# Layer 0's side work placed gap by gap, by the time that each burst of scores leaves

## The chip, the cores and the metric

The kernel runs on one core of a Trainium2 chip, as one program of 39,772 recorded instructions. The metric is the device time of one execution in microseconds (us). It is the median of three runs: 2475.52 us, from 2474.48 to 2475.53.

The engines are TensorE (PE in the profile; PEld is its weight load), VectorE (DVE), ScalarE (ACT), GpSimd (POOL) and SyncE (SP), which issues the DMAs.

## The reference

Four layers of attention run one after the other on `x` (4 batches, 1024 rows, 256 columns, 16 heads of 16) and a context of 77 rows per batch, all in f32. The change is in layer 0, which is causal attention over the layer's own rows and the context, then a feed-forward part:

```python
def _L0_xattn_ref(x, context, ...):
    qkv = (_ln(x, g1, be1) @ w_qkv + b_qkv).reshape(b, t, 3, h, dh)
    ckv = (context @ w_ckv + b_ckv).reshape(b, s, 2, h, dh)
    k = concatenate([k_self, k_ctx], axis=1); v = concatenate([v_self, v_ctx], axis=1)
    scores = where(causal_or_context, einsum('bthd,bshd->bhts', q, k) * scale, -inf)
    x = x + einsum('bhts,bshd->bthd', softmax(scores), v).reshape(b, t, d)
    hdn = gelu(_ln(_ln(x, g2, be2), gf, bf) @ w1 + b1, approximate=False)
    return x + (hdn @ w2 + b2)
```

Layer 1 is a linear attention on the context beside a windowed attention on the rows. Layers 2 and 3 are cross attention to the context, layer 2 with a mask and weights on the scores and a layer norm behind it.

## The kernel before

Layers 0 and 1 work on *units*: four heads of one batch, a "quad", so 16 units a layer. Layer 0 is one call of `step` for each unit (L1634 to L1648). A step runs two things at once: the row maxima of its own unit (`Max0`, eleven items from the table `MAX0`) and the exponentials and sums of the unit before (`Sum0`, twelve items). An item's score products go to a PSUM tile `ps` of two banks. An item has two parts p of two heads each.

`step` (L496) makes a list of bursts of the items: one item of each kind gives two bursts, each with one part of both. A step has 23 bursts, the first step of all (no unit before it) 11. `burst` (L472) issues the products for two `ps` tiles, row by row in turn, then what reads them (`take`): a `tensor_reduce` on DVE into `mpart` (L601) for a `Max0`, an `Exp` on ACT into `pe` (L666) for a `Sum0`, with an `affine_select` on POOL (L669) on the diagonal. The pool `big` holds two `ps` tiles, so a burst can start when both tiles of the burst before it have been read.

Behind each burst comes a *gap*. In it stand, in this order: `sums` of the burst before where it ended an item (products of `pe` and the values into `pv`, L45); what was deferred (transposes `pm` and `pt` of the maxima and of the sums); and a share of the *jobs*. A job is a generator that does one piece of other work for each `next`: `heads0` (queries and keys of the units to come through `project_eight` into `pp`, copied on ACT at L364 and spread by DMA into `qk`), `values0` (`ppv`), `context0`, `ffn` (the feed-forward part of an earlier batch, `ph` and `po`), `ffn_norms`, `features0`, and work for later layers (`folded2`, `keys2`, `heads3`, `keys3`, `folded3`). Each piece takes one or two buffers of the PSUM pool `sm`, which has three.

How far a job has to be is set by `Job.run`: with n pieces and a window a to b of the step, it does pieces until `did` has reached n x (share - a)/(b - a). `share` is how much of the step's sum of `needs` has gone by; a burst's need is a number from its columns, at least 160. All jobs are brought up to the share in the order of the list, so a gap gets as many pieces as fall due there. `jobs0` lists the jobs of each step of layer 0, `jobs1` those of layer 1. The calls to SP's queue (`nc.sync.dma_start`) stand inside the pieces and are issued in the same order.

Layer 1 uses the same `step`, `gap` and `Job`. Layers 2 and 3 use `Job.run` alone, through `gap2`.

Of the kernel before, what the change touches and what calls it, by code (L numbers as in the profile page):

```python
# [31 lines left out]
def tile_xattn_seq(ctx: ExitStack, tc: tile.TileContext, d: dict, out: bass.AP):  # L32
# [8 lines left out]
    sm = ctx.enter_context(tc.tile_pool(name="sm", bufs=3, space=bass.MemoryType.PSUM))  # L41
    pvp = ctx.enter_context(tc.tile_pool(name="pv", bufs=1, space=bass.MemoryType.PSUM))

    def mm(o, lhsT, rhs, start=True, stop=True, **kw):
        nc.tensor.matmul(o, lhsT, rhs, start=start, stop=stop, **kw)  # L45


# [138 lines left out]
            yield  # L186

    ffw = {}

    def load_w1():  # L190
        ffw[1] = wpool.tile([P, 2, FF], F32, name="w1", tag="s3")
# [156 lines left out]
                    )  # L348
                yield None

    def project_eight(st, w, half, xT, bias):

        for q in range(2):
            pp = sm.tile([P, 512], F32, name="pp", tag="sm")
            for c in range(2):
                mm(
                    pp, w[:, c, P * half : P * half + P], xT[:, c, 512 * q : 512 * q + 512],
                    start=(c == 0), stop=(c == 1),
                )
            o = st[:, 512 * q : 512 * q + 512]  # L360
# [75 lines left out]
    class Job:  # L436


        def __init__(self, gen, n, a=0.0, b=1.0, rest=False):
            self.gen, self.n, self.a, self.b, self.did, self.rest = gen, n, a, b, 0, rest  # L440

        def run(self, share):
            want = self.n * min(1.0, max(0.0, (share - self.a) / (self.b - self.a)))
            while self.did < want - 1e-6:
                self.did += 1
                if next(self.gen, StopIteration) is StopIteration:
                    break

        def end(self):
# [35 lines left out]
    def step(items, jobs):  # L485


        bursts = []
        behind = 0
        for m, t in items:  # L490
            cols = max(i.cols for i in (m, t) if i)
            if m and t:
                for p in range(2):
                    bursts.append(((m, p), (t, 1 - p), p and t, cols, p * behind))
            else:
                one = m or t  # L496
                bursts.append(((one, 0), (one, 1), t, 2 * cols, behind if t else 0))
# [12 lines left out]
        for j in jobs:  # L510
            j.end()
# [208 lines left out]
    def heads0(b, half, dst):  # L720


        def begin(quad):
            u = dst[0, b, quad] = new_unit(b, quad)
            u["va"], u["vc"] = vas[half], vcs[b % 2]
            spread(u["kT"][:, 0:S], shared["kc", b][:, half, :], quad % 2)
            return u["qT"], u["kT"][:, S:]

        sts = stage()
        to = begin(2 * half)  # L730
        xT = shared["xT0", b]
        for k in range(2):
            yield from project_eight(
                sts[k], wqk0[:, k], half, xT, bqk0[:, 2 * k + half : 2 * k + half + 1]
            )
# [64 lines left out]
    def ffn(b):  # L800
# [5 lines left out]
        for q in range(5):  # L806
            for half in range(2):
                if q < 4:
                    h = hs[q, half] = work.tile([P, 4, D], F32, name="hT", tag="hT", bufs=3)
                    for f in range(4):  # L810
                        ph = sm.tile([P, D], F32, name="ph", tag="sm")
                        fs = slice(P * (4 * half + f), P * (4 * half + f + 1))
                        for c in range(2):
                            mm(
                                ph, ffw[1][:, c, fs], yT[:, c, D * q : D * q + D],
                                start=(c == 0), stop=(c == 1),
                            )
# [369 lines left out]
    def heads1(b, half, dst):  # L1187
# [13 lines left out]
        to = begin(2 * half)  # L1201
        xT = shared["xT1", b]
        for k, w in enumerate((l1["wq"], l1["wwk"])):
            yield from project_eight(sts[k], w, half, xT, None)
            spread(to[k][:, 0:T], sts[k], 0)
        to = begin(2 * half + 1)
        for k in range(2):
# [319 lines left out]
    def jobs0(b, quad):  # L1527
# [6 lines left out]
            more_places()  # L1534
        if b == 0 and quad == 0:
            j.append(Job(later_constants(), 3, 0.0, 0.4))
            j.append(Job(keep("c00", None), 1, 0.1, 0.2))
# [3 lines left out]
            j.append(Job(values2(), 2, 0.1, 0.2))  # L1541
            j.append(Job(folded2(), 24, 0.2, 1.0))
            j.append(Job(keys2(), 4, 0.5, 0.9))
        if (b, quad) == (0, 1):
            j.append(Job(heads3("wk"), 8, 0.0, 1.0))
        if (b, quad) == (0, 2):
            j.append(Job(keys3(), 16, 0.0, 1.0))
        if (b, quad) == (0, 3):
            j.append(Job(heads3("wv"), 8, 0.0, 1.0))
        if (b, quad) in ((1, 0), (1, 1)):  # L1550
            j.append(Job(keep("f3", folded3), 15 - 6 * quad, 0.0, 1.0, quad == 1))
        if quad == 0 and b + 1 < NB:
            j.append(Job(stats0(b + 1), 8, 0.3 if b == 0 else 0.0, 1.0))
        if quad == 1:
            j.append(Job(values0(b, 1), 4, 0.15, 0.95))
            j.append(Job(keep(("h0", b, 1), lambda: heads0(b, 1, units)), 4, 0.0, 0.85))
            if b:
                j.append(Job(ffn_norms(b - 1), 24, 0.2, 1.0))
        if quad == 2:
# [6 lines left out]
                j.append(Job(features1(0), 8, 0.62, 1.0))  # L1566
        if quad == 3:
            if b + 1 < NB:
                j.append(Job(values0(b + 1, 0), 4, 0.15, 0.9))
                j.append(Job(context0(b + 1), 2, 0.0, 0.4))  # L1570
                j.append(Job(keep(("h0", b + 1, 0), lambda: heads0(b + 1, 0, units)), 4, 0.15, 0.85))
            else:
                j.append(Job(context1(0), 3, 0.3, 0.5))
                j.append(Job(values1(0, 0), 4, 0.4, 0.95))
                j.append(Job(keep(("h1", 0, 0), lambda: heads1(0, 0, units)), 4, 0.45, 0.85))
# [53 lines left out]
    for _ in range(4):  # L1629
        next(run4)  # L1630
    prev = []
    for b in range(NB):
        for quad in range(4):
# [13 lines left out]
            step(pair_up(maxima0(u), prev), jobs0(b, quad))  # L1647
            prev = weights0(u)  # L1648
    shared["st8", 0, 1] = stage()
    for b in range(NB):  # L1650
        for quad in range(4):
            u = units[1, b, quad]
# [96 lines left out]
```

## Time and profile before

| what | value |
|---|---|
| median of three runs | 2475.52 us |
| the profiled execution: its own time | 2472.59 us |
| its span, first to last instruction | 2470.9 us |
| mean granted TensorE clock | 0.972 |
| layer 0's first and last `pe` | 114.1 and 1264.2 us |
| HBM read, written | 57.70 MB, 20.59 MB |

The page's costliest groups (line, engine, operation, output <- input, shapes, count; then busy us, mean ns of one; then the engine's idle time just before them and what ended most of it):

```profile
L45 PE MATMUL ps<-qk 32*128 32x192 f32 (+8 forms) x5760 | 616.5, 468 | 102.1 <-DVE mpart L601 54.4
L666 ACT ACTIVATE pe<-ps 128x1024 f32<-128x1024 f32 (+2 forms) x384 | 363.2, 952 | 612.2 <-PE ps L45 607.0
L601 DVE TENSOR_REDUCE mpart<-ps 128x2 f32<-128x1024 f32 (+3 forms) x448 | 409.0, 933 | 349.1 <-PE ps L45 348.7
```

A line can be that of a helper: all of PE's products but the transposes are recorded at L45, in `mm`. So the tile's name tells what a product is for. "Idle before" of an engine that waits for the bottleneck costs nothing; PE's own idle time does.

### The profile page before, as it was taken

The page shows a single profiled execution, that of the slowest core. Times are in us where ns is not written, and L with a number is a line of the kernel's source. Part 1 is how long each engine was busy: PE and PEld are TensorE (multiplying, and loading weights), DVE is VectorE, ACT ScalarE, POOL GpSimd, SP SyncE. Part 2 cuts the span into 40 slices and gives each one's busy share as a digit, 9 for nine tenths or more (in the row PEclk, how much of TensorE's full clock was granted, in tenths as well). Part 3 has the DMA queues.
Part 4 walks back from the last instruction along what each step waited for, and adds up shares of the span by engine and source line. Part 5 has one row for each costly group of instructions (what it writes and reads, how often), then busy time and mean ns, then how long its engine had stood idle before and what let it go on. Part 6 is the DMA issues. An engine that isn't in the chain of part 4 may idle for free.

```text
span 2470.9 us, 39772 instructions
## 1 busy us (share of the span) xinstructions
PE 2284.0 (92%) x16162; PEld 1376.6 (56%) x16162; DVE 1398.5 (57%) x2347; ACT 1033.3 (42%) x1716; POOL 640.5 (26%) x923
## 2 busy tenths in 40 slices
PE   5789989898998989989999999999997999899999
PEld 3433434344444544445456766666654777788887
DVE  4446456654466444665436345454436899776664
ACT  1244344344344334433453343444444677532222
POOL 2011013111131111311134223333341366643222
PEclk9699999999999999999999999999998999999999
DMA  6402021100000000010000100111104334022200
GB/s 176 115 25 93 6 72 41 45 6 14 1 6 15 6 14 2 5 35 5 14 6 14 19 16 15 19 19 19 19 1 151 124 120 133 28 52 57 54 14 18
DMA packets 87136, 98.49 MB, mean 40 GB/s; under 512 B 31222, under 2 KB 77866, under 8 KB 86826
## 3 DMA queue, kind: packets, MB, share of 16 engines
q1 hardware_dynamic: 86954, 95.95, 14.5%
q8 instruction: 128, 2.10, 0.4%
q14 instruction: 54, 0.44, 0.1%
HBM read 57.70 MB, written 20.59 MB: 32 GB/s over the span
## 4 chain that ended last, share of the span: by engine, by line
PE 78%; DVE 11%; ACT 6%; issue 2%; POOL 1%; DMA 1%; SPq 1%; ACTq 0%; DVEq 0%; POOLq 0%
PE ps L45 33%; PE po L45 15%; PE pp L45 6%; PE pv L45 5%; DVE mpart L601 5%; PE ph L45 4%; PE ppv L45 2%; PE psT L1285 2%; PE pvw L45 2%; ACT pe L666 2%; PE ptx L338 1%; PE pvl L45 1%; PE pk L45 1%; PE pt L542 1%; PE pm L525 1%
## 5 line engine op out<-in xcount | busy, mean ns | idle before, releaser
L45 PE MATMUL ps<-qk 32*128 32x192 f32 (+8 forms) x5760 | 616.5, 468 | 102.1 <-DVE mpart L601 54.4
L666 ACT ACTIVATE pe<-ps 128x1024 f32<-128x1024 f32 (+2 forms) x384 | 363.2, 952 | 612.2 <-PE ps L45 607.0
L601 DVE TENSOR_REDUCE mpart<-ps 128x2 f32<-128x1024 f32 (+3 forms) x448 | 409.0, 933 | 349.1 <-PE ps L45 348.7
L45 PEld LDWEIGHTS ps<-qk 32*128 32x128 f32 (+1 forms) x5760 | 288.2, 185 | 375.0 <-DVE mpart L601 134.1
L45 PE MATMUL po<-U,pT 128*128 128x256 f32 (+1 forms) x1280 | 290.5, 382 | 7.4 <-DVE x L1405 4.7
L45 PEld LDWEIGHTS po<-U,pT 128*128 128x128 f32 (+1 forms) x1280 | 239.8, 191 | 50.0 <-ACT pT L1286 8.0
L669 POOL TENSOR_SCALAR_AFFINE_SELECT pe<-pe 128x256 f32<-128x256 f32 (+1 forms) x192 | 95.0, 495 | 637.0 <-ACT pe L666 636.1
L1056 DVE TENSOR_REDUCE mrow<-ps 128x4 f32<-128x768 f32 x128 | 122.5, 957 | 141.4 <-PE ps L45 141.0
L1286 ACT COPY pT<-psT 128x512 f32<-128x512 f32 (+1 forms) x192 | 92.0, 517 | 228.1 <-PE psT L1285 228.0
L1131 ACT ACTIVATE pew<-ps 128x768 f32<-128x768 f32 x128 | 103.4, 811 | 173.4 <-PE ps L45 172.6
L1136 POOL TENSOR_SCALAR_AFFINE_SELECT pew<-pew 128x512 f32<-128x512 f32 x128 | 81.6, 637 | 342.0 <-ACT pew L1131 342.0
L45 PE MATMUL pv<-pe,va 128*32 128x512 f32 (+3 forms) x1536 | 165.0, 518 | 0.1
L45 PE MATMUL ps<-G,xT 128*128 128x308 f32 x512 | 143.0, 423 | 0.0
L45 PE MATMUL ph<-yT,w 128*128 128x256 f32 x512 | 138.1, 405 | 0.8 <-DVE qk L527 0.8
L1366 ACT ACTIVATE s<-s,nm 128x77 f32<-128x77 f32 x512 | 131.2, 352 | 15.9 <-DVE nm L1399 15.9
L1498 POOL TENSOR_TENSOR s<-s,den 128x1232 f32<-128x1232 f32 x32 | 72.0, 2249 | 207.7 <-DVE den L1497 192.4
L45 PEld LDWEIGHTS ph<-yT,w 128*128 128x128 f32 x512 | 93.6, 198 | 52.6 <-issue 39.1
L45 PE MATMUL po<-w,hT 128*128 128x256 f32 x512 | 117.0, 382 | 0.0
L45 PEld LDWEIGHTS ps<-G,xT 128*128 128x128 f32 x512 | 92.4, 190 | 26.8
L45 PEld LDWEIGHTS po<-w,hT 128*128 128x128 f32 x512 | 95.4, 190 | 21.0 <-issue 9.1
L527 DVE TENSOR_TENSOR qk<-pm,qk 128x512 f32<-128x512 f32 x64 | 44.0, 688 | 105.2 <-PE pm L525 105.2
L818 DVE TENSOR_SCALAR hT<-ph,c_L_xattn_b 128x256 f32<-128x256 f32 x128 | 61.3, 480 | 72.4 <-PE ph L45 65.2
(191 smaller groups left out, 3175.7 us busy)
## 6 DMA issues: line engine op xcount, KB each, us to landing
side<-in_fside_t SPq DMA_DIRECT2D x32, 616.0 KB
qk<-st SPq DMA_DIRECT2D x256, 64.0 KB
U<-kept_u SPq DMA_DIRECT2D x8, 1152.0 KB
side<-in_mask_t SPq DMA_DIRECT2D x32, 154.0 KB
G<-kept_g SPq DMA_DIRECT2D x4, 1232.0 KB
x<-in_x SPq DMA_DIRECT2D x8, 512.0 KB
out<-x SPq DMA_DIRECT2D x32, 128.0 KB
kept_u<-st SPq DMA_DIRECT2D x21, 154.0 KB
```

Source lines behind the costliest of these rows:

```text
L45: nc.tensor.matmul(o, lhsT, rhs, start=start, stop=stop, **kw)
L601: nc.vector.tensor_reduce(mpart[bl][:, i, 2 * p : 2 * p + 2, ci], ps[:, :, o : o + w], axis=AX.X, op=ALU.max,)
L666: nc.scalar.activation(pp[:n, :, o:512], ps[:n, :, o:512], AF.Exp, scale=SC)
L669: nc.gpsimd.affine_select(out=own, in_=own, compare_op=ALU.is_ge, fill=0.0, base=0, pattern=[[0, 2], [0, k], [1, P]], channel_multiplier=-1,)
L818: nc.vector.tensor_scalar(h[:, f, :], ph, cols["L0_xattn_b1"][:, 4 * half + f : 4 * half + f + 1], None, ALU.add,)
L1056: nc.vector.tensor_reduce(mo, ps.rearrange("p j (i n) -> p j i n", i=2)[:, :, :, 0 : P + WIN], axis=AX.X, op=ALU.max, negate=True,)
L1131: nc.scalar.activation(pp[:, :, :, 0 : P + WIN], ps.rearrange("p j (i n) -> p j i n", i=2)[:, :, :, 0 : P + WIN], AF.Exp, scale=SC,)
L1136: nc.gpsimd.affine_select(out=pf[:, :, 0:P], in_=pf[:, :, 0:P], compare_op=ALU.is_ge, fill=0.0, base=0, pattern=[[0, 4], [1, P]], channel_ ...
L1285: nc.tensor.transpose(ps[:, k, :], s[:, P * c : P * c + P], ident)
L1286: nc.scalar.copy(pT[:, 4 * group : 4 * group + n, :], ps[:, 0:n, :])
L1366: nc.scalar.activation(hs, hs, AF.Exp, bias=p1["nm"][:, h : h + 1], scale=SC)
L1498: nc.gpsimd.tensor_tensor(s3, s3, den.unsqueeze(2).to_broadcast([P, H, S]), ALU.mult)
```

## The change

Layer 0's jobs that use PE get a cost of one piece in us (`us=`); the others keep `us=0` and run as before. `mm` counts what was put on PE, in `put`, as columns / 600. `step` works out, where there are jobs with a cost, how long each burst's tiles are read beyond what stands in the gap anyway (`reads`), and raises or lowers all of them by one amount `lo` so that they sum to the work of the jobs. Each gap then takes pieces with a cost in `fill`: always the job that is furthest behind, in us, until nothing is behind or the gap's time is used up; a job that is more than two pieces and 1 us behind is served anyway. What a gap leaves over or overdraws goes to the next through `left`.

Two kinds of piece are halved in layer 0: `project_eight` works on 256 columns in place of 512 (8 pieces per `heads0` in place of 4; layer 1 keeps 512), and the second product of `ffn` on 128 columns in place of 256, with its own add on DVE for each half; `whole` turns this off once layer 1 begins.

```diff
+    put = [0.0]
     def mm(o, lhsT, rhs, start=True, stop=True, **kw):
+        n = 1
+        for k in rhs.shape[1:]:
+            n *= k
+        put[0] += n / 600.0
         nc.tensor.matmul(o, lhsT, rhs, start=start, stop=stop, **kw)
...
-    def project_eight(st, w, half, xT, bias):
-        for q in range(2):
-            pp = sm.tile([P, 512], F32, name="pp", tag="sm")
+    def project_eight(st, w, half, xT, bias, n):
+        for q in range(T // n):
+            pp = sm.tile([P, n], F32, name="pp", tag="sm")
...
+        def late(self, share):
+            want = self.n * min(1.0, max(0.0, (share - self.a) / (self.b - self.a)))
+            return want - self.did
+        def piece(self):
+            self.did += 1
+            return next(self.gen, StopIteration) is not StopIteration
...
         for j in jobs:
-            j.run(share)
+            if not j.us:
+                j.run(share)
+    def fill(share, jobs, until):
+        while True:
+            due = [(j.late(share) * j.us, -i) for i, j in enumerate(jobs) if j.us and j.did < j.n]
+            late, i = max(due, default=(-1.0, 0))
+            if late <= 1e-6:
+                break
+            j = jobs[-i]
+            if late < 2.0 * j.us + 1.0 and put[0] + 0.5 * j.us > until:
+                break
+            if not j.piece():
+                j.did = j.n
...
-        needs = [max(160.0, 140 + cols - 0.8 * filled) for *_, cols, filled in bursts]
-        total, at = sum(needs), 0.0
-        for (*parts, t, _, _), need in zip(bursts, needs):
+        work = sum(j.n * j.us for j in jobs)
+        if work:
+            reads = [0.3 + n * (0.1 + c / 455.0) - f / 600.0 for *_, n, c, f in bursts]
+            lo, hi = -3.0, 30.0
+            for _ in range(40):
+                more = (lo + hi) / 2
+                if sum(max(0.0, r + more) for r in reads) > work:
+                    hi = more
+                else:
+                    lo = more
+            needs = [max(0.0, r + lo) for r in reads]
+        else:
+            needs = [max(160.0, 140 + n * c - 0.8 * f) for *_, n, c, f in bursts]
+        total, at, left = sum(needs), 0.0, 0.0
+        for (*parts, t, _, _, _), need in zip(bursts, needs):
             burst([(i, p, pair_tile()) for i, p in parts])
             if t and pending:
                 pending.pop(0)()
             at += need
+            left += need
+            was = put[0]
             gap(at / total, jobs)
+            fill(at / total, jobs, was + left)
+            left -= put[0] - was
...
-                        po = sm.tile([P, D], F32, name="po", tag="sm")
-                        for f in range(8):
-                            mm(
-                                po, h2[f // 4][:, f % 4, P * i : P * i + P], ffw[2][:, f, :],
-                                start=(f == 0), stop=(f == 7),
-                            )
-                        nc.vector.tensor_tensor(xq, po, xq, ALU.add)
-                        nc.gpsimd.tensor_tensor(xq, xq, rows["b2"], ALU.add)
-                        for _ in range(4):
-                            yield
+                        n = D if whole else P
+                        for a in range(0, D, n):
+                            po = sm.tile([P, n], F32, name="po", tag="sm")
+                            for f in range(8):
+                                mm(
+                                    po, h2[f // 4][:, f % 4, P * i : P * i + P],
+                                    ffw[2][:, f, a : a + n], start=(f == 0), stop=(f == 7),
+                                )
+                            nc.vector.tensor_tensor(xq[:, a : a + n], po, xq[:, a : a + n], ALU.add)
+                            if a + n == D:
+                                nc.gpsimd.tensor_tensor(xq, xq, rows["b2"], ALU.add)
+                            for _ in range(n // 64):
+                                yield
...
-            j.append(Job(values0(0, 0), 4, 0.2, 0.8))
+            j.append(Job(values0(0, 0), 4, 0.2, 0.8, us=0.85))
...
-            j.append(Job(keep(("h0", b, 1), lambda: heads0(b, 1, units)), 4, 0.0, 0.85))
+            j.append(Job(keep(("h0", b, 1), lambda: heads0(b, 1, units)), 8, 0.0, 0.85, us=0.85))
...
-                j.append(Job(keep(("ffn", fb), lambda: ffn(fb)), n, a, 0.97, last))
+                j.append(Job(keep(("ffn", fb), lambda: ffn(fb)), n, a, 0.97, last, us=0.85))
```

The other jobs of `jobs0` get their `us` in the same way: `folded2`, `folded3` and the first context 0.85, `context0` 0.9, `values2` 1.0, `keys2` 0.5, `heads3` and `keys3` 1.03, `heads1` (four pieces still) 1.7. Without a cost stay `stats0`, `features0`, `ffn_norms`, `ffn_features`, `stats1`, `features1`, `context1`, the constants, and the last piece of `heads0`, which loads the keys of the next unit in the first gap of every second step.

More of the change, by code (lines that the diff above doesn't have):

```diff
@@ L188, in tile_xattn_seq @@
     ffw = {}
+    whole = []
     def load_w1():
@@ L349, in to_features @@
                 yield None
-    def project_eight(st, w, half, xT, bias):
-        for q in range(2):
-            pp = sm.tile([P, 512], F32, name="pp", tag="sm")
+    def project_eight(st, w, half, xT, bias, n):
+        for q in range(T // n):
+            pp = sm.tile([P, n], F32, name="pp", tag="sm")
             for c in range(2):
                 mm(
-                    pp, w[:, c, P * half : P * half + P], xT[:, c, 512 * q : 512 * q + 512],
+                    pp, w[:, c, P * half : P * half + P], xT[:, c, n * q : n * q + n],
                     start=(c == 0), stop=(c == 1),
                 )
-            o = st[:, 512 * q : 512 * q + 512]
+            o = st[:, n * q : n * q + n]
             if bias is None:
@@ L436, in tile_xattn_seq, with __init__ @@
     class Job:
-        def __init__(self, gen, n, a=0.0, b=1.0, rest=False):
+        def __init__(self, gen, n, a=0.0, b=1.0, rest=False, us=0.0):
             self.gen, self.n, self.a, self.b, self.did, self.rest = gen, n, a, b, 0, rest
+            self.us = us
+        def late(self, share):
[4 more added lines that the diff above has]
+            return next(self.gen, StopIteration) is not StopIteration
         def run(self, share):
[L443 to L446, printed above, removed]
+            while self.late(share) > 1e-6:
+                if not self.piece():
                     break
@@ L493, in step @@
                 for p in range(2):
-                    bursts.append(((m, p), (t, 1 - p), p and t, cols, p * behind))
+                    bursts.append(((m, p), (t, 1 - p), p and t, 1, cols, p * behind))
             else:
                 one = m or t
-                bursts.append(((one, 0), (one, 1), t, 2 * cols, behind if t else 0))
+                bursts.append(((one, 0), (one, 1), t, 2, cols, behind if t else 0))
             if t:
                 behind = t.cols
-        needs = [max(160.0, 140 + cols - 0.8 * filled) for *_, cols, filled in bursts]
-        total, at = sum(needs), 0.0
-        for (*parts, t, _, _), need in zip(bursts, needs):
+        work = sum(j.n * j.us for j in jobs)
[13 more added lines that the diff above has]
+        for (*parts, t, _, _, _), need in zip(bursts, needs):
             burst([(i, p, pair_tile()) for i, p in parts])
@@ L733, in heads0 @@
             yield from project_eight(
-                sts[k], wqk0[:, k], half, xT, bqk0[:, 2 * k + half : 2 * k + half + 1]
+                sts[k], wqk0[:, k], half, xT, bqk0[:, 2 * k + half : 2 * k + half + 1], D
             )
@@ L1203, in heads1 @@
         for k, w in enumerate((l1["wq"], l1["wwk"])):
-            yield from project_eight(sts[k], w, half, xT, None)
+            yield from project_eight(sts[k], w, half, xT, None, 512)
             spread(to[k][:, 0:T], sts[k], 0)
@@ L1536, in jobs0 @@
             j.append(Job(later_constants(), 3, 0.0, 0.4))
-            j.append(Job(keep("c00", None), 1, 0.1, 0.2))
-            j.append(Job(values0(0, 0), 4, 0.2, 0.8))
+            j.append(Job(keep("c00", None), 1, 0.1, 0.2, us=0.85))
+            j.append(Job(values0(0, 0), 4, 0.2, 0.8, us=0.85))
             j.append(Job(other_contexts(), 3, 0.0, 0.1))
             j.append(Job(feature_weights(), 3, 0.5, 1.0))
-            j.append(Job(values2(), 2, 0.1, 0.2))
-            j.append(Job(folded2(), 24, 0.2, 1.0))
-            j.append(Job(keys2(), 4, 0.5, 0.9))
+            j.append(Job(values2(), 2, 0.1, 0.2, us=1.0))
+            j.append(Job(folded2(), 24, 0.2, 1.0, us=0.85))
+            j.append(Job(keys2(), 4, 0.5, 0.9, us=0.5))
         if (b, quad) == (0, 1):
-            j.append(Job(heads3("wk"), 8, 0.0, 1.0))
+            j.append(Job(heads3("wk"), 8, 0.0, 1.0, us=1.03))
         if (b, quad) == (0, 2):
-            j.append(Job(keys3(), 16, 0.0, 1.0))
+            j.append(Job(keys3(), 16, 0.0, 1.0, us=1.03))
         if (b, quad) == (0, 3):
-            j.append(Job(heads3("wv"), 8, 0.0, 1.0))
+            j.append(Job(heads3("wv"), 8, 0.0, 1.0, us=1.03))
         if (b, quad) in ((1, 0), (1, 1)):
-            j.append(Job(keep("f3", folded3), 15 - 6 * quad, 0.0, 1.0, quad == 1))
+            j.append(Job(keep("f3", folded3), 15 - 6 * quad, 0.0, 1.0, quad == 1, us=0.85))
         if quad == 0 and b + 1 < NB:
@@ L1554, in jobs0 @@
         if quad == 1:
-            j.append(Job(values0(b, 1), 4, 0.15, 0.95))
-            j.append(Job(keep(("h0", b, 1), lambda: heads0(b, 1, units)), 4, 0.0, 0.85))
+            j.append(Job(values0(b, 1), 4, 0.15, 0.95, us=0.85))
+            j.append(Job(keep(("h0", b, 1), lambda: heads0(b, 1, units)), 8, 0.0, 0.85, us=0.85))
             if b:
@@ L1568, in jobs0 @@
             if b + 1 < NB:
-                j.append(Job(values0(b + 1, 0), 4, 0.15, 0.9))
-                j.append(Job(context0(b + 1), 2, 0.0, 0.4))
-                j.append(Job(keep(("h0", b + 1, 0), lambda: heads0(b + 1, 0, units)), 4, 0.15, 0.85))
+                j.append(Job(values0(b + 1, 0), 4, 0.15, 0.9, us=0.85))
+                j.append(Job(context0(b + 1), 2, 0.0, 0.4, us=0.9))
+                j.append(Job(keep(("h0", b + 1, 0), lambda: heads0(b + 1, 0, units)), 8, 0.15, 0.85, us=0.85))
             else:
                 j.append(Job(context1(0), 3, 0.3, 0.5))
-                j.append(Job(values1(0, 0), 4, 0.4, 0.95))
-                j.append(Job(keep(("h1", 0, 0), lambda: heads1(0, 0, units)), 4, 0.45, 0.85))
+                j.append(Job(values1(0, 0), 4, 0.4, 0.95, us=0.85))
+                j.append(Job(keep(("h1", 0, 0), lambda: heads1(0, 0, units)), 4, 0.45, 0.85, us=1.7))
         for fb, n, a, last in (
@@ L1628, in tile_xattn_seq @@
     run4 = keep(("h0", 0, 0), lambda: heads0(0, 0, units))
-    for _ in range(4):
+    for _ in range(8):
         next(run4)
@@ L1649, in tile_xattn_seq @@
     shared["st8", 0, 1] = stage()
+    whole.append(True)
     for b in range(NB):
```

## The prediction

> **What bounds the kernel now.** I read the page first, then the waits of TensorE (PE) between 115 and 1200 us, which is layer 0 without its start, then the timeline of PE there, then short windows for the clock.
>
> ```profile
> span 2470.9 us, 39772 instructions
> ...
> PE 2284.0 (92%) x16162; PEld 1376.6 (56%) x16162; DVE 1398.5 (57%) x2347; ACT 1033.3 (42%) x1716; POOL 640.5 (26%) x923
> ...
> PE   5789989898998989989999999999997999899999
> ...
> PEclk9699999999999999999999999999998999999999
> ```
>
> PE bounds the kernel; no other engine reaches 60%. The second half of PE's row is nines; layer 0 (slices 3 to 20) is a mix of eights and nines. There lies what can be won: 1085 us of which PE is busy 985 (first line of the last fence).
>
> ```profile
> PE ps L45 <- DVE mpart L601: 54.4, 82, 1.3
> PE ps L45 <- DMA qk<-st: 15.1, 5, 3.8
> PE ps L45 <- ACT pe L666: 15.1, 26, 0.9
> ```
>
> Columns: us in total, times, longest. A burst of scores writes two `ps` tiles, and the `big` pool holds two, so the next burst waits until VectorE (DVE) has reduced the one and ScalarE (ACT) or DVE has read the other. 70 of the 100 us that PE idles are this wait. The timeline shows what decides it:
>
> ```profile
> 426.28 1.14 PE L45 MATMUL ps<-qk 32*128 32x512 f32 x8
> 427.35 1.06 PE L45 MATMUL pv<-pe,va 128*32 128x512 f32 x8
> 428.73 1.14 PE L45 MATMUL ps<-qk 32*128 32x512 f32 x8 [0.32 <-DVE mpart L601]
> 429.80 0.70 PE L45 MATMUL pu<-l3wo,kv 64*128 64x256 f32 x4
> 430.44 1.16 PE L45 MATMUL ppv<-s,xT 128*128 128x128 f32 x8
> 431.52 1.14 PE L45 MATMUL ps<-qk 32*128 32x512 f32 x8
> 432.60 1.06 PE L45 MATMUL pv<-pe,va 128*32 128x512 f32 x8
> 434.30 1.14 PE L45 MATMUL ps<-qk 32*128 32x512 f32 x8 [0.64 <-DVE mpart L601]
> 436.75 2.09 PE L45 MATMUL ps<-qk 32*128 32x512 f32 x8 [1.31 <-DVE mpart L601]
> 438.77 1.67 PE L45 MATMUL pv<-pe,va 128*32 128x512 f32 x8
> ```
>
> Start to start of two bursts is 2.45 us with nothing between them (434.30 to 436.75, idle 1.31), 2.45 with one `pv` of 0.9 us (426.28 to 428.73, idle 0.32), and 2.79 with `pu` and `ppv` (428.73 to 431.52, idle none). So about 1.2 us of other work per gap is free, what is missing is lost as idle time, and what goes beyond it is paid in full. The same work, spread evenly, costs less.
>
> ```profile
> 115.00:1200.00 1085.00, 985.07 (x6952) 463.23 (x6951) 591.81 (x978) 439.18 (x509) 176.64 (x296) 0.97 0.09 23
> 433.20:436.60 3.40, 1.60 (x16) 0.31 (x8) 2.68 (x4) 1.59 (x2) 0.00 (x0) 1.00 0.11 36
> 436.60:440.00 3.40, 3.25 (x16) 0.72 (x16) 2.23 (x6) 1.04 (x2) 0.41 (x1) 0.50 0.00 0
> 580.00:586.80 6.80, 6.40 (x22) 2.11 (x24) 1.27 (x2) 1.67 (x2) 0.00 (x0) 0.50 0.00 0
> ```
>
> After the us and the busy times of PE, PEld, DVE, ACT and POOL come the granted clock, the DMA share and GB/s. After 3.4 us in which PE idled 1.8, the clock is halved for the next 3.4. Between 115 and 1200 us this happens 15 times, 72 us in all, which costs up to 36.
>
> **Term 1: the gaps.** The bursts are the same, in the same order, in both programs. From the order of PE's instructions in each I took, for the 330 gaps of the fifteen steps after the first (without each step's first gap), the time that the filler streams for: 0.429 us per pass of 512 columns, 0.216 of 256, 0.111 of 128, the median start-to-start times of `pp`, `po` and `ppv` in the trace (an f32 product takes two passes; four `pv` on four column strips count as one). The sum is the same before and after, 442.5 and 443.7 us, since no job leaves its step; only its spread changes. For before I set beside each gap its excess: the time from one burst's start to the next's, less the streaming of burst and filler. By filler:
>
> - none: 38 gaps before, 11 after; median excess 1.43 us
> - 0.4 to 0.6 us: 30 and 19; 0.99
> - 0.8 to 1.1: 122 and 139; 0.70
> - 1.2 to 1.5: 35 and 36; 0.57
> - 1.7 to 2.3: 66 and 102; 0.61
> - 2.6 and more: 39 and 23; 0.60
>
> The last four differ little: there the excess is the fixed cost of changing over. Differences times excess: -38.6 - 10.9 + 11.9 + 0.6 + 22.0 - 9.6 = **-24.6**. By PE's idle alone (means 1.07, 0.47, 0.12, 0.03, 0.09, 0.05) it is -29.7. Taking each gap as the larger of its read-bound period (1.9 to 2.6 us by place in the step) and burst plus filler plus a fixed 0.35 to 0.75, it is -32 to -20. I take -25, bounds -32 and -20.
>
> **Term 2: the clock.** Of the 15 halvings three follow gaps that were empty and have 0.9 to 1.75 us after (those at 436.6 and 665.3) or a fuller neighbour (1040.8); 3.4 us at half speed each, so 1.7 us of loss each: -5 if all go. Five follow the wait for `qk` at a unit's start, two the transposes that wait for `xn`, five lie beside Gelu. Gelu blocks ACT for 4.6 us (a table load of 1.28, two activations of 1.0, a load of 1.28), which holds the exponentials back and costs 2 to 5 us two bursts later, ten times. The filler between the Gelu and that burst is the same or alike (3.05 us and 3.05 in three of the ten places), so I leave these. If the 580.0 and 883.8 halvings, whose window also holds an empty gap, go too, that is 7 more (2 x 6.8 us at half speed). Halvings can also arise where a window falls otherwise. I take -4, bounds -12 and +5.
>
> [...]
>
> **Term 3: the halves.** 144 of 256 `po` products of 256 columns become 288 of 128, 64 `pp` products of 512 become 128 of 256. A pass of `po` then costs 2 x 0.111 - 0.216 = 0.006 more, for 288 passes 1.7 us; `pp`, 2 x 0.216 - 0.429 = 0.003 for 128 passes, 0.4. The weight load of each pass stays hidden, as the 0.111 of `ppv`, with a fresh load each, shows. From above: `ppv` takes 1.08 us for 8 passes with its tail (430.44 to 431.52), a 256-column `po` 3.65 us for 16 in its row at 668.79; by these a half costs 0.042 more a pass, 12 us. I take +2, since the tail is already in the excess.
> [...] The trace's 111, 216 and 429 are proportional to the columns, so I go by them.
> Other engines: DVE gets 18 more adds (at most 0.42 each, L836: 7.6 us), ACT 32 more evictions (at most 0.69, L364: 22 us). DVE is busy 592 of 1085 us and ACT 439, and both wait for PE, so I cost this at nothing; with that cover gone it is up to 30.
>
> **What moves past queues.** No DMA is added. The loads of the next unit's keys stand in the last piece of `heads0`, which still runs in the first gap of an even step, and the filler of that gap is the same in both programs (0.53, 0.44, 0, 0, 0 us in the five that wait); the 3 to 3.8 us that PE waits there stay. The `qk` transfers of the first half of `heads0` go out after the fourth of eight pieces, as before after the second of four; the stores of `kept_u`, `kept_g` and `kept_k` follow their pieces on SP's queue, as many as before. POOL's adds of `b2` stay one per row block, 928 instructions in both. In the first step DMA is the limit (PE busy 76 of the first 115 us), the pieces per gap are alike, but the staging buffers are taken in another order: 0, bounds -3 and +3. Layer 1's jobs carry no cost, so it keeps its old spread.
>
> **Sum.** -25 - 4 + 2 = -27. The profiled execution took 2472.6 us (span 2470.9), 2.9 below the median of the runs, 2475.5; so the forecast is 2445.6 on its own scale and **2448.5** as a median.
>
> **Rivals.**
> - Half of it: the filler that fills empty gaps sends its evictions to DVE, ahead of a reduce; where each of the 27 newly filled gaps loses one eviction of 0.42 us (11 in all) and the clock gives nothing, 25 - 11 - 2 leaves 12: 2463. For it: DVE's queue is in order. Against: gaps with 1.7 us and more already have these evictions and no larger excess.
> - More: the large bounds of terms 1 and 2 together, -32 - 12 + 2: 2433. Against: the Gelu blocks stay.
> - Nothing: the pieces are too coarse to fit, 2475. Against: empty gaps fall from 38 to 11 in the program itself.
> - Slower: the `sm` pool. It has three buffers, and gaps with three or more of its tiles rise from 31 to 43, with two from 68 to 74. A piece that waits for a buffer waits for an eviction behind a reduce, 1.22 + 0.48 = 1.7 us, with the next burst queued behind it on PE. If all 43 paid it, +73 against -27: 2521; it decides from 0.63 us each. At 1 us: 2491. Against: before, gaps with three such tiles have a median excess of 0.61, with one 0.61.
>
> **Chances.** Forecast 0.58, half 0.19, more 0.06, nothing 0.05, slower 0.12. A measurement of this kernel tells 0.2% (5 us) from no change; so faster 0.83, same 0.05, slower 0.12. The forecast's own range, each term half-way to its bounds (-34 to -15), is 2441 to 2460. The range of 8 in 10 reaches up past the half case to the edge of no change and down to the larger gain: 2431 to 2474.
>
> **What would show it.** Right: between 115 and 1170 us PE's wait on `mpart` falls from 54 to about 25 us; the `qk` waits stay at 15 to 19; layer 0's last `pe` ends about 27 us earlier than 1264; layers 1 to 3 keep their lengths. Wrong: `po` halves starting further apart than 0.12 us a pass, new waits of `pp`, `ph` or `po` on evictions, or more than 15 halvings of the clock in layer 0.

## The result, and the profile after

| kernel | median of four runs | lowest to highest |
|---|---|---|
| before | 2475.00 us | 2474.01 to 2475.53 |
| after | 2443.89 us | 2442.25 to 2447.61 |

The ratio is 0.9881, with a 95% interval from 0.9868 to 0.9895: 31 us faster. The profiled execution of after took 2442.25 us, 30.3 less than that of before. Layer 0's last `pe` ends at 1233.4 us instead of 1264.2; what comes behind it takes 1207.1 us, before 1206.6. So the whole gain lies in layer 0. The half-clock stretches that the prediction counted as 15 between 115 and 1200 us are 11 between 115 and 1170 us in after.

The page of after: span, the engines' busy time, PE's row and its clock in 40 slices.

```profile
span 2440.5 us, 40648 instructions
...
PE 2279.2 (93%) x16578; PEld 1418.9 (58%) x16578; DVE 1402.0 (57%) x2365; ACT 1040.1 (43%) x1748; POOL 639.8 (26%) x923
...
PE   5799989899998999899999999999998999999999
...
PEclk9799999999999999999999999999998999999999
```

PE has more products and is busy 4.8 us less, since less of it runs at half clock (51.2 us between 115 and 1170 us, 71.7 before); the eights of layer 0 (slices 3 to 20) have become fewer. The waits of PE between 115 and 1170 us in after (us in total, times, longest):

```profile
PE ps L51 <- DVE mpart L650: 22.1, 55, 1.3
PE ps L51 <- ACT pe L715: 15.0, 23, 1.8
PE ps L51 <- DMA qk<-st: 11.4, 4, 3.6
PE ps L51 <- issue: 11.0, 2, 9.3
```

In the same window before had 53.1, 14.4 and 15.1 us for the first three. The wait on the row maxima's reduce has gone to 22.1, the one on the exponentials has not moved. The fourth line, a wait whose end the profile puts down to nothing, was 1.7 us before: one of 9.3 us is new. The timeline of PE in after, at the place that the prediction showed of before:

```profile
420.56 1.14 PE L51 MATMUL ps<-qk 32*128 32x512 f32 x8 [0.32 <-DVE mpart L650]
421.63 1.13 PE L51 MATMUL pp<-xT,wqk 128*128 128x256 f32 x4
422.69 0.70 PE L51 MATMUL pu<-l3wo,kv 64*128 64x256 f32 x4
423.32 1.14 PE L51 MATMUL ps<-qk 32*128 32x512 f32 x8
424.39 1.07 PE L51 MATMUL pv<-pe,va 128*32 128x512 f32 x8
425.78 1.14 PE L51 MATMUL ps<-qk 32*128 32x512 f32 x8 [0.32 <-DVE mpart L650]
426.85 1.13 PE L51 MATMUL pp<-xT,wqk 128*128 128x256 f32 x4
428.23 1.14 PE L51 MATMUL ps<-qk 32*128 32x512 f32 x8 [0.25 <-DVE mpart L650]
```

Each gap now holds some filler, a half `pp` of 256 columns for instance, and the idle times are 0.3 us, where before an empty gap cost 1.31.

**Where the time went.** For the fifteen steps after the first I split the time from the first burst of the first of them to the first burst behind the last into four parts. Idle is time without a PE record, in the first gap of each step and outside it. The loss to the clock is half of the time in which the granted clock was 0.5 and PE not idle. The rest is what is left: streaming and the changes from burst to filler. In us:

| kernel | 15 steps | idle outside the first gaps | idle in the first gaps | loss to the clock | rest |
|---|---|---|---|---|---|
| before | 1089.4 | 78.1 | 21.9 | 36.9 | 952.6 |
| after | 1057.6 | 47.0 | 27.6 | 24.5 | 958.4 |
| difference | -31.8 | -31.1 | +5.8 | -12.3 | +5.8 |

Of the +5.8 in the rest 1.2 is streaming (750.5 to 751.7 us by the prediction's price per pass).

### The profile page after: what moved, and what is told of

It reads as the page before. It is cut to its first block, busy times and chain, and to the rows that moved or that the text cites. A ratio compares the mean times of both kernels' runs of the same rounds, so it can differ in the third digit from the quotient of the medians.

```text
span 2440.5 us, 40648 instructions
## 1 busy us (share of the span) xinstructions
PE 2279.2 (93%) x16578; PEld 1418.9 (58%) x16578; DVE 1402.0 (57%) x2365; ACT 1040.1 (43%) x1748; POOL 639.8 (26%) x923
## 4 chain that ended last, share of the span: by engine, by line
PE 79%; DVE 10%; ACT 6%; issue 2%; POOL 2%; DMA 1%; SPq 1%; ACTq 0%; DVEq 0%; POOLq 0%
PE ps L51 33%; PE po L51 16%; PE pp L51 6%; PE pv L51 5%; DVE mpart L650 5%; PE ph L51 4%; PE ppv L51 2%; PE psT L1338 2%; PE pvw L51 2%; PE ptx L345 2%; PE pvl L51 1%; PE pk L51 1%; PE pt L591 1%; PE pu L51 1%; PE pm L574 1%
## 5 line engine op out<-in xcount | busy, mean ns | idle before, releaser
L51 PE MATMUL ps<-qk 32*128 32x192 f32 (+8 forms) x5760 | 608.2, 464 | 76.5 <-DVE mpart L650 22.1
L51 PE MATMUL pv<-pe,va 128*32 128x512 f32 (+3 forms) x1536 | 159.8, 504 | 0.0
L51 PE MATMUL po<-w,hT 128*128 128x128 f32 (+1 forms) x800 | 124.6, 310 | 0.0
L51 PEld LDWEIGHTS po<-w,hT 128*128 128x128 f32 x800 | 110.0, 193 | 20.4 <-issue 13.8
L51 PEld LDWEIGHTS ph<-yT,w 128*128 128x128 f32 x512 | 94.1, 197 | 38.6 <-issue 24.5
L51 PEld LDWEIGHTS <-identb 128*128 128x128 bf16 x576 | 33.1, 97 | 104.4 <-issue 100.3
```

## The experiments

Times are medians; each label's ratio is against runs of the kernel before on the same chip (2472.1 to 2474.4 us).

**The halves alone.** The jobs run by share as before, with the old needs; the halved pieces stay.

```diff
         for j in jobs:
-            if not j.us:
-                j.run(share)
+            j.run(share)
...
-        work = sum(j.n * j.us for j in jobs)
+        work = 0.0
...
             gap(at / total, jobs)
-            fill(at / total, jobs, was + left)
```

> The halved pieces stay, the placing is taken out: every job runs by its share in list order as in the kernel before, with the old needs. Counted in the order of PE's instructions, 18 gaps are empty (before 38, changed kernel 11) and 31 hold 2.6 us and more (39 and 23). By the excess of each class of gap that is -17 us against before, -4 for the clock: 2454. Theory of the prediction (a gain is what the evener spread gives, by whatever means): 2450 to 2460. Rival (the halves are only a tool of the placing, alone they do nothing): 2475.

Measured: 2440.74 us, ratio 0.9883 (0.9855 to 0.9912), as fast as the whole change. Both theories missed. The parts: idle outside the first gaps 56.6 us, in them 21.9, clock 25.8, rest 952.7. The waits of PE in this kernel, between 115 and 1170 us:

```profile
PE ps L51 <- DVE mpart L648: 38.3, 66, 1.3
PE ps L51 <- DMA qk<-st: 15.2, 5, 3.7
```

The placing takes another 16 us from the first line and 9.6 from the idle time, and gives it all back in the first gaps (5.7 us) and in the rest (5.7).

**The placing alone.** The gaps are filled by their times, but in whole pieces (`pp` of 512, `po` of 256 columns).

```diff
-    whole = []
+    whole = [True]
...
-                sts[k], wqk0[:, k], half, xT, bqk0[:, 2 * k + half : 2 * k + half + 1], D
+                sts[k], wqk0[:, k], half, xT, bqk0[:, 2 * k + half : 2 * k + half + 1], 512
```

The jobs of `heads0` have four pieces of 1.7 us again.

> The placing stays, the halves are taken out: pp on 512 columns (4 pieces of 1.7 us), po on 256. 17 gaps are empty, 35 hold 2.6 us and more. By the classes -16 us, less some 5 for the longer wait for qk at 440 us that the changed kernel shows: theory 2455 to 2464. Rival (placing does it all, the halves add only instructions): 2444 or less.

Measured: 2453.22 us, 0.9937 (0.9911 to 0.9962): 1.8 us below the theory's range, and the rival is refuted. Idle outside the first gaps is 55.8 us, that of the halves alone; in the fifteen steps the halves win 32.4 us, the placing 21.5 and both together 31.8, so the two work on the same idle time and don't add up. Of the 10.9 us that the placing wins less than the halves, 5.7 are the longer first gaps, in which the new wait of 9.3 us stands here too.

**Even gaps.** Every burst gets the same allowance of reading time, whatever it reads.

```diff
-            reads = [0.3 + n * (0.1 + c / 455.0) - f / 600.0 for *_, n, c, f in bursts]
+            reads = [1.0 for _ in bursts]
```

> Halves and the most belated job first stay, but each gap gets the same time, whatever its burst leaves to be read and whatever already stands in it. 24 gaps are empty, 30 hold 0.4 to 0.6 us, 97 hold 0.8 to 1.1. By the classes -13 us against before: theory 2460 to 2466. Rival (how the time is dealt out does not matter, only that pieces are not bunched): 2444.

Measured: 2459.81 us, 0.9961 (0.9943 to 0.9978), 0.2 us below the expected range. So how the times follow the reads matters, by 16 us: idle outside the first gaps is 9.1 us more than in after, in them 5.1, and the clock costs 7.4 more.

**In the list's order.** The gap's time is filled with what is due first in the list, not with the most belated job.

```diff
-            due = [(j.late(share) * j.us, -i) for i, j in enumerate(jobs) if j.us and j.did < j.n]
-            late, i = max(due, default=(-1.0, 0))
+            due = [
+                (j.late(share) * j.us, -i) for i, j in enumerate(jobs)
+                if j.us and j.did < j.n and j.late(share) * j.us > 1e-6
+            ]
+            late, i = due[0] if due else (-1.0, 0)
```

> As the changed kernel, but of the jobs that are behind the first of the list is served, not the most belated. The classes are nearly the same (11, 22, 140, 36, 95, 26), -22 us against -23.5: theory 2445, within 4 us of the changed kernel. Rival (the order among jobs keeps pieces from waiting for each other's buffers and evictions): 2455 or more.

Measured: 2445.11 us, 0.9905 (0.988 to 0.9931). The order of the most belated is worth nothing that these runs can tell. In this kernel the new wait of 9.3 us is absent (its longest wait on `qk` is 3.8 us), the first gaps idle 4.9 us less than in after, and the clock costs 6.7 more.

**The weights later.** The new wait of 9.3 us stands in the first gap of step 6 (batch 1, quad 2). The timelines of SP's queue (SPq) and of the bursts there, first before, then after:

```profile
441.63 0.30 SPq L921 DMA_DIRECT2D kept_u<-st  x1
442.03 0.41 SPq L74 DMA_DIRECT2D w<-in_L_xattn_w  x1
442.62 0.40 SPq L74 DMA_DIRECT2D wout<-in_L_xattn_Wout  x1
...
447.88 1.10 PE L45 MATMUL ps<-qk 32*128 32x461 f32 x8
...
448.95 2.41 SPq L371 DMA_DIRECT2D qk<-st  x4
...
452.79 0.62 PE L45 MATMUL ps<-qk 32*128 32x461 f32 x1 [3.81 <-DMA qk<-st]
```

```profile
438.47 1.10 PE L51 MATMUL ps<-qk 32*128 32x461 f32 x8
439.10 0.30 SPq L974 DMA_DIRECT2D kept_u<-st  x1
439.50 0.41 SPq L80 DMA_DIRECT2D w<-in_L_xattn_w  x1
440.09 0.39 SPq L80 DMA_DIRECT2D wout<-in_L_xattn_Wout  x1
440.58 2.41 SPq L379 DMA_DIRECT2D qk<-st  x4
...
448.90 1.87 PE L51 MATMUL ps<-qk 32*128 32x461 f32 x5 [9.33 <-issue]
```

The loads of `w1` and `wout` (1024 and 512 KB) stand behind the last store of `kept_u`. Before, that store came 6 us ahead of the step's first burst. In after the placing has put `folded3`'s last `pu` into the last gap of the step before, so the store comes behind the burst, and the loads directly ahead of the keys. The share of the 16 DMA engines in 40 slices, before from 440 to 453 us, then after from 438 to 450:

```profile
DMA  0000000353957899999999981000000929292821
```

```profile
DMA  0000003599098985699999999989598640001010
```

Before, the loads are through by 448.1 us (25 slices of 0.325), ahead of the keys' transfers, issued at 448.95. In after the engines are busy with loads and keys until 447.9 (33 slices of 0.3). The packets of the trace, by size and count, tell the order: the 256 of 4 KB of `w1` start first, the last at 444.6 us; the 64 of 4 KB of the first four keys' transfers start from 445.2 to 447.7, though these were issued from 440.58 on. So the keys stand behind the loads more than beside them. Before, the keys' first packet started 1.2 us after its issue, in after 4.7. The edit puts the two loads behind the keys, as a job of their own in the step's list:

```diff
+        if (b, quad) == (1, 2):
+            j.append(Job(weights_of_ffn(), 1, 0.0, 0.01))
...
-            if (b, quad) == (1, 2):
-                load_w1()
-                load_wout()
```

> As the changed kernel, but the loads of w1 (1024 KB) and wout (512 KB) at the start of the step of batch 1, quad 2 are issued behind the qk loads of that step's first gap, not ahead of them. Theory: in the changed kernel they waited for the last piece of folded3, which the placing pushed into the last gap of the step before, and so ran beside the qk loads; PE waited 9.3 us where it waited 3.8 before. Then the wait falls to 3 to 4 us and 3.4 us at half clock go: 2437. Rival (the wait is long for another reason, such as the qk loads' own wait for the buffer): 2444, wait still 9 us.

Measured: 2442.22 us, 0.9869 (0.9855 to 0.9882), in time between theory and rival, and the wait is 3.66 us, that of before:

```profile
443.10 2.41 SPq L379 DMA_DIRECT2D qk<-st  x4
...
446.79 2.64 PE L51 MATMUL ps<-qk 32*128 32x461 f32 x8 [3.66 <-issue]
...
453.72 0.59 SPq L80 DMA_DIRECT2D w<-in_L_xattn_w  x1
```

So the cause of the stall is settled, but the total moved by 1.6 us, not 6. The first gaps idle 5.6 us less than in after; the clock costs 7.1 more, with 6.8 us at half speed in step 7, where after had none. (The profiled execution, of 2444.99 us, was the slowest of the four.) I ran this kernel once more:

> The same kernel as the one with the weight loads behind the key loads (2442.2 us, four runs), once more with more runs and a second profile. In its first profile the stall was 5.6 us shorter, but the clock was halved 11 us longer than in the changed kernel's, 6.8 of it in steps 1 to 5, where the two programs have the same order. Theory: the halvings differ from one execution to the next, since the windows fall otherwise; a second profile has another list of them, step 7 need not lose 3 us again, and with more runs the median lies 2 to 6 us below the changed kernel's 2443.8: 2438 to 2442. Rival: the edit itself moves a halving into step 7, which again takes about 73 us and not 70, and the median stays at 2442 to 2444.

Measured: 2442.86 us, 0.9886 (0.9866 to 0.9907), from 2438.93 to 2449.04. Step 7 took 73.2 us again with 6.8 at half speed, so the rival holds, for that and for the median: some 3 of the 5.6 us are given back to the clock there. Of the theory only the first half holds: the halvings between the first step and layer 0's end come to 61.4 us in the first profile and 51.2 in the second, of one program, and the profiled executions took 2444.99 and 2438.93. That one pair differs by 6 us, the clock's loss by 4.2 (31.6 and 27.4); another 2.0 lie ahead of the fifteen steps.

**The keys early.** The key loads for the next unit are the last piece of `heads0`, which runs in the first gap of the step that needs them. The edit makes them a piece by themselves, one gap or more ahead.

```diff
             spread(to[k][:, 0:T], sts[k], 0)
+        yield
         to = begin(2 * half + 1)
...
-            j.append(Job(keep(("h0", b, 1), lambda: heads0(b, 1, units)), 8, 0.0, 0.85, us=0.85))
+            j.append(Job(keep(("h0", b, 1), lambda: heads0(b, 1, units)), 9, 0.0, 0.85, us=0.85))
```

The other job of `heads0`, and the first units ahead of the steps, get a ninth piece in the same way.

> As the changed kernel, but heads0 yields once more after it has issued the loads of the keys, so that these go out in the step before and not in the first gap of the step that needs them (9 pieces for 8). PE's waits in the first gaps of the even steps (27.6 us of idle in the changed kernel, 9.3 of it in one) should go, and with them the halvings of the clock behind them. Theory (those waits are lost time on PE's path): -22 to -33 us, 2411 to 2422. Rival (the time only moves to the exponentials or the maxima, which are read from the same buffer): 2435 to 2444.

Measured: 2417.28 us, 0.9769 (0.9756 to 0.9783): 26.6 us less than the changed kernel run beside it, and within the theory. PE's waits between 115 and 1170 us:

```profile
PE ps L51 <- DVE mpart L650: 28.5, 65, 1.2
PE ps L51 <- ACT pe L715: 17.4, 25, 1.8
...
PE ps L51 <- DMA qk<-st: 1.9, 2, 1.7
```

The waits on the keys are gone but for 1.9 us. By the parts the first gaps idle 6.2 us (27.6 in after) and the clock costs 11.4 (24.5); idle elsewhere is 4 more. The clock is now halved only in the first gap of step 1 and in the three bursts behind four of the Gelus: in all other gaps 0.2 us at half speed, in after 33.8. Of these 33.8 us, 27 belong to halvings that begin 3 to 7 us after a step's first burst, directly behind the stall, and went with it. The other two halvings of after (781.2 and 1040.6 us, 3.4 us each) stand behind shorter waits (1.26 and 0.78 us). Whether they went with the stalls or because the halvings fell otherwise in this execution is not shown.

**No Gelu**, and **the changed kernel again**, beside these. The first leaves out the Gelu:

```diff
-                                nc.scalar.activation(hs[q, k], hs[q, k], AF.Gelu)
+                                nc.scalar.activation(hs[q, k], hs[q, k], AF.Identity)
```

> As the changed kernel, with Identity in place of Gelu in the feed-forward part of layer 0: it leaves out the activation, and with it the two table loads on ACT around each pair. It measures what the prediction left in place: Gelu's blocks of 4.6 us on ACT, ten in layer 0's steps and six in layer 1's. Theory (each block holds the exponentials and costs PE about 2 us two bursts later, and half of the remaining halvings lie beside it): -20 to -35 us, 2409 to 2424. Rival (the filler beside them hides it): 2438 to 2444.

> The changed kernel beside these three on the same chip: 2444.

Measured: 2420.35 us, 0.9779 (0.9766 to 0.9792), and 2443.84 us, 0.9876 (0.9863 to 0.9889). The first lies within the theory. ScalarE at one Gelu of the changed kernel, then at the same place without it:

```profile
570.20 1.28 ACT L873 ACT_TABLE_LOAD   x1
571.50 2.00 ACT L873 ACTIVATE hT<-hT 128x1024 f32<-128x1024 f32 x2
573.52 1.28 ACT L715 ACT_TABLE_LOAD   x1
```

```profile
569.90 2.07 ACT L873 ACTIVATE hT<-hT 128x1024 f32<-128x1024 f32 x2
571.87 1.01 ACT L715 ACTIVATE pe<-ps 128x1024 f32<-128x1024 f32 x1
```

The two activations stay, at the same 1.05 us each; what goes is the table loads, two around each pair. So the 23.5 us are the price of the loads and not of the whole 4.6 us block: 22.3 in the fifteen steps, which hold ten of the pairs, and 1.1 behind them, where the other six stand. Behind the places of the Gelus no halving is left, in after 10.2 us.

**The halves with early keys, the kernel before with early keys, and cover for the Gelu.** The first is the kernel of "the halves alone", the second the kernel before, each with the `yield` shown above. The third is the kernel with early keys, with pieces taken before they are due in the gap in which a Gelu was issued:

```diff
                                 nc.scalar.activation(hs[q, k], hs[q, k], AF.Gelu)
+                            cover[0] = 2.5
...
+        while cover[0] > 0.0:
+            open_ = [
+                (j.late(share) * j.us, -i) for i, j in enumerate(jobs)
+                if j.us and j.did < j.n and share > j.a
+            ]
+            if not open_:
+                break
+            j = jobs[-max(open_)[1]]
+            cover[0] -= j.us
+            j.piece()
+        cover[0] = 0.0
```

> The changed kernel without its placing (halves alone, 2440.7 us as measured) and with the key loads of the next quad one piece earlier, which took 26.6 us from the changed kernel (2443.8 to 2417.3). Theory: the placing saved about 7 us of idle time behind late readers (44.2 against 37.4 us outside the first gaps) and lost it in the first gaps, where the weight loads fell beside the key loads; with the key loads out of the way only the saving is left, so halves and early keys come to 2423 to 2430 us, with the waits on the partial sums back near 38 us. Rival: the placing is worth nothing on top of the halves, and the kernel comes to 2417 or below.

> The kernel before, neither halves nor placing, with only the key loads of the next quad one piece earlier. Theory: the stalls of 3 to 4 us in the first gap of the later even steps go (15 to 19 us of waits on the key transfers) and the halvings of the clock that begin in them (8 to 12 us), and this adds to what the change gives: 2443 to 2452 us. Rival: those halvings are set off by any of the unfilled gaps, and go only where the gaps are filled as well: 2455 to 2462 us.

> The changed kernel with early keys (2417.3 us), and in the gap in which a Gelu is issued some 2.5 us of matmul pieces more, taken before they are due, most belated first. The Gelu holds the exponentials up and some 20 us near the ten of them are left (without Gelu: 23.5 us less). Theory: the wait is covered where the pieces lie ahead of it, 2405 to 2414 us. Rival: the pieces are only taken from the gaps behind, which then stand empty (17 empty gaps by the order of the instructions against 11), and it costs as much there: 2417 to 2425 us.

Measured: 2420.32 us, 0.9799 (0.9775 to 0.9824); 2445.48, 0.9901 (0.9879 to 0.9923); 2409.61, 0.9758 (0.9737 to 0.9778).

The first lies between theory and rival. By the parts the placing takes 11.8 us of idle time from it (62.8 to 51.0) and the rest takes back 8.1 (951.7 to 959.8). The 3 us by which early keys with the placing are faster are not secured, as the intervals of the two kernels overlap. The second is within the theory: early keys take 26.6 us (2472.11 to 2445.48) from the kernel before too, as much as from the changed one within the interval (19 to 30 us). So the stalls at the start of the even steps and what the change does are independent as far as these runs tell, and one `yield` is worth nearly as much as the whole change. The rival is not quite dead: three halvings of 6.8 us each are left in the middle of a step here (451.3, 744.8 and 1038.4 us). Each begins during a wait of 1.5 us of the transposes for `xn`. None stands at an empty gap, though PE's wait on the maxima's reduce (62.5 us) shows that these remain.

The third is the fastest kernel of the study, though not by the mechanism that I named. It was not run beside the one with early keys: by the medians it is 7.7 us faster, by the ratios 2.7, and the intervals overlap; in the two profiles the fifteen steps take 9.3 us less. Idle time is what it was (51.9 and 51.0 us): the wait on the exponentials falls from 17.4 to 7.7 us, that on the maxima's reduce rises from 28.5 to 37.4. The clock's loss falls from 11.4 to 4.5, the rest by 3.2. The same place in both, first with early keys alone:

```profile
555.76 2.00 ACT L874 ACTIVATE hT<-hT 128x1024 f32<-128x1024 f32 x2
...
557.79 1.28 ACT L715 ACT_TABLE_LOAD   x1
...
560.16 1.13 PE L51 MATMUL ps<-qk 32*128 32x512 f32 x4 [1.84 <-ACT pe L715]
561.21 2.05 PE L51 MATMUL ppv<-s,xT 128*128 128x128 f32 x8
```

```profile
555.13 1.05 PE L51 MATMUL ppv<-s,xT 128*128 128x128 f32 x8
556.02 1.03 PE L51 MATMUL ph<-yT,w 128*128 128x256 f32 x4
...
556.25 2.00 ACT L886 ACTIVATE hT<-hT 128x1024 f32<-128x1024 f32 x2
...
559.43 4.65 PE L51 MATMUL ps<-qk 32*128 32x512 f32 x16 [0.32 <-DVE mpart L662]
...
564.01 1.06 PE L51 MATMUL pv<-pe,va 128*32 128x512 f32 x8
```

In the first, `ps` waits 1.84 us for the exponentials behind the Gelu and its table loads, and the `ppv` behind it takes 2.05 us, where it takes 1.16 at full clock (432.01 us of after). In the second there is more filler ahead (`ppv` and `ph`), two bursts stand in one row, and the `pv` behind them runs at its full 1.06 us. ACT is held up for as long as in the first; what changed is that the clock is not halved. Which of the two, the filler ahead or another fall of the halvings, keeps it up is not shown.

## Why the prediction was right

The forecast of 2448.5 lies 4.6 us above the median and the mechanism is the one it named: the same bursts, a more even filler. By its terms:

- **Term 1, the gaps, -25.** Measured: -31.1 us of idle time outside the first gaps (the working by idle alone gave -29.7) and +4.6 in the rest beyond the streaming, together -26.5. The excess per class counts both, which is why its -24.6 was the better sum. The method did as well on the even gaps (13 us by the classes and 13.0 measured) and on the list's order (2445 and 2445.1), but not on the halves alone: with 18 empty gaps they would win 17 us, and 4 from the clock, and they won 21.5 and 11.1 in the fifteen steps. Why is open.
- **Term 2, the clock, -4.** Mis-sized: -12.3, at the bound of -12. The prediction left in the halvings beside Gelu because the filler there was alike; in the three bursts behind each, half-speed time fell from 27.3 to 10.2 us. The three halvings behind empty gaps (436.6, 665.3, 1040.8) have no counterpart in after, as predicted. In all the gaps that are neither first nor behind a Gelu it fell from 42.7 to 33.8, and in the first gaps it rose from 6.3 to 12.2. The prediction did name that halvings can arise elsewhere; the runs show how much that is: of the four runs of after one took 2442.4 us at a mean clock of 0.976 and one 2447.6 at 0.970. By these, a clock term read from one profile is not known better than by some 5 us.
- **Term 3, the halves, +2.** The passes of `po` start 0.112 us apart and those of 256 columns 0.216, as predicted, and by these prices the streaming grew by 1.2 us. The halves alone left the rest of the fifteen steps where it was (952.6 and 952.7 us). So the upper bound of 0.042 a pass, 12 us, is refuted. DVE's halved adds are 0.292 us each, not 0.42. I named -25 as coming from the spread, which fits; that halved pieces in the old order are as fast as the whole change (2440.7 us), though they leave 18 gaps empty and not 11, was not in the prediction. Without early keys the placing adds nothing to them that these runs can tell.
- **What moves past queues.** Here is a step that failed: "the stores of `kept_u` ... follow their pieces on SP's queue, as many as before" was true, and I stopped there. (POOL's instructions are 923 by the pages of both, not 928.) The loads of `w1` and `wout` wait behind the last of these stores and came to stand directly ahead of the keys: +5.6 us in one gap. The other four waits on `qk` stayed (15.1 us before, 11.4 in after for four), as predicted.
- **The sum.** -26.5 - 12.3 + 1.2 + 5.8 = -31.8 for -27: a clock term 8 too small and a stall not seen partly cancel. That the total lies closer than its terms is luck in part.

Of the rivals, "half of it" (2463) fails: the newly filled gaps do not pay for evictions, the wait on `mpart` fell below the 25 us forecast. (That DVE held to its order can be seen at one place of before: it idled 1.55 us ahead of the reduce at 616.33 us, and the statistic of `x` at 617.43, whose rows were loaded at the start, came behind.) "More" (2433) had the clock right, but the gaps gave 26.5 us and not 32, and the stall was not in it. "Slower", the `sm` pool, fails: new waits of `pp`, `pu` and `ppv` come to 1.9 us in all over layer 0, against the 27 (43 gaps of 0.63) from which it decided.

What lies beyond the change: early keys make it 2417.3 us, and cover for the Gelu 2409.6, 2.4% below the runs of before beside it.

## What to carry to other kernels

Before planning where each piece goes, halve the pieces: a finer grain in the old order gave the time of the planner here, though not its even gaps (56.6 us of idle time outside the first gaps, and 47.0). After a reordering, follow every queue to what is issued behind the moved instructions, even if they are as many as before, and look at which transfers then run at the same time. And a stall can cost more than its length where the clock drops behind it (without the stalls on the keys the first gaps idled 21.4 us less, and the loss to the clock was 13.1 less): look for stalls of 3 us at fixed places first, since one `yield` that ended them won 26.6 us from either kernel.

## What the runs showed of the hardware

- One program can get another list of halvings in another execution: 61.4 and 51.2 us in two profiles of the kernel with later weights. It need not: the two profiles of the changed kernel have the same eleven halvings, of the same lengths, some 1.7 us apart (183.8 and 185.6 us the first, 1040.6 and 1042.4 the last).
- In each of the two traces, before and after, the halvings lie on a grid: the shortest last 3.413 us by the trace's clock records, the longer ones between 115 and 1170 us two or three times that, and all begin whole multiples of 3.413 us apart (within 0.01 us). The last five of after in the fifteen steps, for instance, begin at 781.2, 866.5, 928.0, 1030.4 and 1040.6 us, which are 25, 18, 30 and 3 times 3.413 apart. With the stalls at the steps' starts gone, 0.2 us of halving was left in the gaps that are neither first nor behind a Gelu in the changed kernel, but 20 us in the kernel before, at waits of 1.5 us. That it is the idle time in the stretch before that sets a halving off fits the one that the prediction showed (1.8 us of idle in the 3.4 before 436.6 us), but was not tried by itself.
- The f32 passes of layer 0 start 0.112, 0.216 and 0.429 us apart for 128, 256 and 512 columns (medians of `ppv`, `po` and `pp`), in proportion to the columns within 5%, each with a fresh weight load. Halving the tiles alone moved the rest of the fifteen steps by 0.1 us.
- One store issued 2.5 us earlier (441.63 and 439.10), but on the other side of a burst, made a wait of 3.8 us one of 9.3: the keys' transfers then stand behind 1.5 MB that nothing needs yet, and their first packet started 4.7 us after its issue, where it had been 1.2.
- The table loads around ten pairs of Gelu, 20 of 1.28 us on ScalarE, cost the fifteen steps 22.3 us; the activations themselves stayed in the kernel that showed it.
